# Softmax sums gathered by a longer chain of accumulating transfers, and a round's first two scores placed around its first transposed ones

## The chip, the cores and the metric

The kernel runs on one core of a Trainium2 chip. The metric is the device time of one execution in microseconds, as the median of several executions. The profile comes from one further execution; its instructions' span is a little shorter than that execution's time.

In the profile, PE is the matrix engine (PEld its weight loads), DVE the vector engine, ACT the scalar engine, POOL the GpSimd engine and SP the engine that issues most transfers.

## The reference

One pre-norm block over `x` of shape (2, 2048, 512), in float32: attention with 16 heads of 32 and two groups of keys and values, and then a feed-forward product with values rounded to an 8-bit format.

```python
x = x + attn(layernorm(x))
x = x + ffn(layernorm(x))

# attn: q, k with rotary positions
scores = einsum('bqhd,bkhd->bhqk', q * hd ** -0.5, k_exp) * hd ** -0.5
attn = softmax(scores, axis=-1)
out = einsum('bhqk,bkhd->bqhd', attn, v_exp).reshape(b, s, d)
return out @ wo + bo

# ffn: both operands rounded to e4m3 with one scale each
acc = matmul(x_fp8, w_fp8.T); return (acc * (sx * sw)).astype(bfloat16)
```

What matters here is the softmax: for each query and head, the maximum over 2048 keys, the exponentials, their sum over the keys, and the sum of values weighted by them.

## The kernel before

The tokens are cut into 8 blocks of 512 (four to a batch). A front part normalizes the first batch, projects its keys and values and the first queries. Then comes the attention loop, which takes nearly all of the time, and at the end the rounded product.

**Units.** The attention loop runs over 64 units. A unit is one block, one quad of four heads, and one half (256) of the block's queries. It runs in four rounds, and a round takes four chunks of 128 keys. The order of all instructions on each engine is the order of the program text (`tc.manual_schedule()`); nothing is reordered.

**Scores for the maxima (L517, L524).** A generator makes, for a later unit, plain scores `s` with queries on the partitions: 32 matmuls of 128x512 a unit, each followed by a maximum on DVE into `part`. Each call of `next(scores)` makes two. It runs eight scores ahead (`LEAD`), so a unit's loop makes the last 24 of the next unit's scores in its first three rounds, and the first eight of the unit after that in its last. The `s` tiles go round three banks of PSUM, of which one is at times lent to other work. After a unit's 32nd score the maxima are gathered (L531, L532), split into two parts on POOL (L503), and turned by PE (L542) ahead of the columns of chunk 14.

**Transposed scores and exponentials (L954, L963, L972).** In `probabilities`, PE makes transposed scores `T` (keys on the partitions, four heads of 256 queries) in two alternating banks, "E" and "O". In chunks 0 and 1 it first puts the negative maxima there by a selection matrix. `T` holds in later chunks only the difference of keys between chunks, added on top. ACT takes the exponential `p` (L972), in four buffers.

**Weighted values (L913).** `columns` multiplies the four chunks' `p` by the values, 16 matmuls a round, into one half of the bank `avs`.

**Sums of exponentials.** POOL adds the `p` of two chunks (`add_pair`, L946): the first two give `pair`, the last two a tile `pa` that is kept as `far_sums[r]`, with one buffer for each of the four rounds. A transfer that adds to its destination, issued by POOL (L1015), puts `pair` onto `far_sums[r]`; in the third round a second one (L1017) puts `far_sums[0]` onto `far_sums[1]`. In the next unit PE sums over the 128 partitions with a matrix of ones (`sum_up`, L927), into the other half of `avs`: `far_before[1:3]` at the end of the first round, `far_before[3:]` at the end of the second.

**End of the heads.** After the second `sum_up`, `finish_heads` is put into the list `finishing`. As a job it is stepped once when it is made, which has ACT copy the sums into `both[:, 1]` (L885). Its two reciprocals on DVE (L889) and the product on POOL (L890), which reads both halves of `both`, follow when `fill(ON_DVE)` reaches it, in the round after. The unit ends with ACT copying the weighted values into `both[:, 0]`:

```python
both = w2.tile([P, 2, HB], F32, tag="both", name=f"both_{u}", bufs=1)
nc.scalar.copy(both[:, 0, :], avs[:, 0, :])
far_before = far_sums
```

`both` has one buffer. In the next unit's text, ACT first has, in every other unit, a cast of queries (`hi_q`, L246, whose other half `lo_q` POOL makes, L247), and then the first exponentials.

**Other work.** Projections of keys and queries, the output product, the second normalization and the weight's rounding are jobs that `fill` steps between a round's parts: `fill(ON_PE)` after a round's second pair of scores (not in the first round) and ahead of its last pair, `fill(ON_DVE)` ahead of the columns.

Of the kernel before, what the change touches and what calls it, by code (L numbers as in the profile page):

```python
# [13 lines left out]
ALU = mybir.AluOpType  # L14
# [13 lines left out]
def preln_attn_fp8_ffn_kernel(  # L28
# [37 lines left out]
    nc = tc.nc  # L66
# [10 lines left out]
    HT = HB // P  # L77
    HALVES = TB // HB
    ROUND = 4
    ROUNDS = NTS // ROUND  # L80
    LEAD = 4

    ON_PE, ON_DVE, OTHER = "PE", "DVE", "other"
    LATER = "later"
# [24 lines left out]
    def s_bank():  # L109

        if s_next[0] == lent[0]:
            s_next[0] = (s_next[0] + 1) % S_BANKS
        tag = f"s{s_next[0]}"
        s_next[0] = (s_next[0] + 1) % S_BANKS
        return tag
# [354 lines left out]
    units = [(k, half) for k in range(len(quads)) for half in range(HALVES)]  # L470
# [23 lines left out]
    def group(k):  # L494
        return quads[k][1] // (QUADS // GROUPS)
# [11 lines left out]
    def scores_for_maxima():  # L507

        for u, (k, half) in enumerate(units):
            part = small.tile([P, HT, 4, NKB], F32, tag="part", name=f"part_{u}", bufs=3)  # L510

            order = [(i, kb) for i in range(HT) for kb in range(NKB)]
            for i, kb in order if u else sorted(order, key=lambda at: at[1]):
                for j in range(4):
                    s = ps_s.tile([P, TB], F32, tag=s_bank(), name=f"s_{u}_{i}_{kb}_{j}")
                    at = (half * HT + i) * P
                    nc.tensor.matmul(  # L517
                        s,
                        qst[k][:, j, at : at + P],
                        stacked["kS"][:, group(k), kb * TB : (kb + 1) * TB],  # L520
                        start=True,
                        stop=True,
                    )
                    nc.vector.tensor_reduce(part[:, i, j, kb : kb + 1], s, AX.X, ALU.max)  # L524
                    if j == 1:
                        yield u
                if (i, kb) == (HT - 1, NKB - 1):

                    mview = mrow.rearrange("p (i j r) -> p i j r", i=HT, j=4)
                    mx = small.tile([P, HT, 4], F32, tag="mx", name=f"mx_{u}")  # L530
                    nc.vector.tensor_reduce(mx, part, AX.X, ALU.max)  # L531
                    nc.scalar.copy(mview[:, :, :, 0], mx)  # L532
                    split.append((mview, mx))
                yield u
# [139 lines left out]
    def run(steps):  # L674
        for _ in steps:
            pass
# [4 lines left out]
    def together(*runs):  # L681

        live = list(runs)
        while live:
            for steps, n in list(live):
                for _ in range(n):
                    if next(steps, "end") == "end":
                        live.remove((steps, n))
                        break
# [9 lines left out]
    MIDDLE = DC + 1  # L699
    QUERIES = DC + 2  # L700
    scores = scores_for_maxima()
    PART = HT * 2
    with tc.manual_schedule():
        xnT = {
            0: wide_block("xnT", "xnT_kv_0"),
# [17 lines left out]
        kv[3] = project_kv(3, x_kv[3], xnT[3], load_tables(3))  # L723
        together((first(kv[3], FRONT), 2), (first(scores, PART), 1))
        together((first(kv[3], MIDDLE), 1), (first(scores, PART), 1))
        together((kv[3], 1), (first(scores, PART), 1))
        run(first(scores, PART))
        gather_maxima(0, ps_s.tile([P, TB], F32, tag=s_bank(), name="mtp_0"))
# [176 lines left out]
    def columns(u, chunks, probs, av):  # L905

        k, half = units[u]
        for kc, p in zip(chunks, probs):
# [3 lines left out]
            for j in range(4):  # L912
# [7 lines left out]
                    skip_group_check=True,  # L920
                )

    def sum_up(dst, parts, start, stop):

        for i, part in enumerate(parts):
            for j in range(4):
                nc.tensor.matmul(  # L927
                    dst[j * HD : (j + 1) * HD, :],
                    ones,
                    part[:, j, :],  # L930
                    start=start and i == 0,
                    stop=stop and i == len(parts) - 1,
                    tile_position=(0, j * HD),
                    skip_group_check=True,
                )
# [13 lines left out]
    def probabilities(u, T, kc):  # L949

        k, half = units[u]
        if kc < 2:
            for j in range(4):
                nc.tensor.matmul(  # L954
                    T[:, j, :],
                    sel[:, j, :],
                    maxima[u],
                    start=(j % 2 == 0),
                    stop=True,
                    skip_group_check=True,  # L960
                )
        for j in range(0, 4, 2):
            nc.tensor.matmul(  # L963
                T[:, j : j + 2, :],
                stacked["dkS"][:, group(k), kc * P : (kc + 1) * P],
                qst[k][:, j : j + 2, half * HB : (half + 1) * HB],
                start=False,
                stop=True,
                skip_group_check=True,
            )  # L970
        p = ppool.tile([P, 4, HB], F32, tag="p", name=f"p_{u}_{kc}")
        nc.scalar.activation(p, T, AF.Exp, scale=SCALE)  # L972
        return p

    with tc.manual_schedule():
        for _ in range(LEAD):
            next(scores)
        for u, (k, half) in enumerate(units):
            n, quad = quads[k]
            if half == 0 and quad == 0:  # L980
                attn_of[n] = wide.tile(
                    [P, QUADS, TB], F32, tag="attn", name=f"attn_{n}", bufs=2
                )
            stack_next(u)
            banks = [
                ps_t.tile([P, 4, HB], F32, tag="EO"[parity], name=f"T_{u}_{parity}")
                for parity in range(2)
            ]

            far_sums = []  # L990
            whole = u == len(units) - 1
            ending_soon = u >= len(units) - 2
            pieces = 2 if ending_soon else 1
            for r in range(ROUNDS):
                chunks = list(range(r * ROUND, (r + 1) * ROUND))
                step[0] += 1
                while r == 1 and landing:
                    landing.pop()()
                if r == 2:
                    ask(u)  # L1000
                last = r == ROUNDS - 1
                next(scores, None)
                probs = [probabilities(u, banks[kc % 2], kc) for kc in chunks[:2]]
                pair = add_pair(u, chunks[0], *probs)
                next(scores, None)
                if r > 0:
                    fill(ON_PE, pieces)
                probs.append(probabilities(u, banks[0], chunks[2]))
                next(scores, None)
                probs.append(probabilities(u, banks[1], chunks[3]))  # L1010
                if ending_soon:
                    fill(ON_DVE)
                if not (last and whole):
                    far_sums.append(add_pair(u, chunks[2], *probs[2:]))
                    nc.gpsimd.dma_start(out=far_sums[r], in_=pair, accum_op=ALU.add)  # L1015
                if r == 2:
                    nc.gpsimd.dma_start(out=far_sums[1], in_=far_sums[0], accum_op=ALU.add)  # L1017
                fill(ON_PE, pieces)
                next(scores, None)
                split_maxima()  # L1020
                fill(ON_DVE, 3 if finishing else 2)
                if r == 0:
                    avs = ps_av.tile([P, 2, HB], F32, tag="av", name=f"avs_{u}")
                columns(u, chunks, probs, avs[:, 0, :])


                if u > 0 and r == 0:
                    sum_up(avs[:, 1, :], far_before[1:3], False, False)
                elif u > 0 and r == 1:
                    sum_up(avs[:, 1, :], far_before[3:], False, True)  # L1030
                    finishing.append(Job(finish_heads(u - 1, both, avs[:, 1, :])))
            both = w2.tile([P, 2, HB], F32, tag="both", name=f"both_{u}", bufs=1)
            nc.scalar.copy(both[:, 0, :], avs[:, 0, :])
            far_before = far_sums
        sums = ps_s.tile([P, TB], F32, tag=s_bank(), name="sums_last")[:, :HB]
        sum_up(sums, [pair, *probs[2:], *far_sums[1:]], True, True)
        finishing.append(Job(finish_heads(u, both, sums)))
        fetch_y_over_keys(2, "kS", 1)
        attending[0] = False
        for jobs in (finishing, queue, beside):  # L1040
            while jobs:
                jobs[0].step()
                if jobs[0].kind is None:
                    jobs.pop(0)
# [55 lines left out]
    with tc.manual_schedule():  # L1100
# [5 lines left out]
        for at, (n, i) in enumerate(tiles):  # L1106
            if i % 2 == 0 and at + AHEAD < len(tiles):
                m, j = tiles[at + AHEAD]
# [58 lines left out]
```

## Time and profile before

| what | value |
|---|---|
| median of 3 runs | 2333.15 us (2331.62 to 2337.78) |
| the profiled execution | 2336.02 us |
| its span, first to last instruction | 2334.2 us |
| mean granted TensorE clock | 0.970 |
| L524 maxima on DVE | 1304.2 us, x2048 of 684 ns |
| L972 exponentials on ACT | 1001.4 us, x1024 of 1024 ns |
| L517 scores on PE | 832.1 us, x2048 |
| L963 transposed scores on PE | 669.5 us, x2048 |
| L913 weighted values on PE | 509.4 us, x8192 |
| L890 product on POOL | 85.2 us, x64 of 1331 ns |
| queue 0 (POOL's transfers) | 175.66 MB, 40.0% of 16 engines |
| queue 1 (SP's transfers) | 133.21 MB, 19.2% |
| transfers pa<-pa, issue to landing | median 4.9 us, longest 16.3 |

A row of groups gives the line, the engine, the operation, what it writes and reads, the count; then busy time and the mean of one; then the idle time of the engine just before and what ended it. In a timeline, the columns are the start, the length, the engine and the line, with idle time before it in brackets. A matmul on float32 values leaves two records. Records of POOL may overlap: an instruction can start before the record of the one ahead has ended.

### The profile page before, as it was taken

To read this page: it belongs to the slowest core of one execution; us is meant where nothing else is said; L and a number is where in the kernel's file an instruction comes from. 1 tells how busy PE (TensorE), PEld (TensorE's weight loads), DVE (VectorE), ACT (ScalarE), POOL (GpSimd) and SP (SyncE) were. 2 spreads that over 40 slices of the span, in tenths; PEclk is the share of its full clock that TensorE was granted. 3 is DMA by queue.
4 is the path that set the end of the run, shared out by engine and by line. 5 is a ranking of instruction groups with operands and counts; after the bars stand their busy time and mean duration, and the time that the engine had idled before them with its cause. 6 is when DMAs were issued, how large, how long until landed. Compare 5 with 4: busy or idle time off the path is not lost. (4 is left out here: it accounts for less than half of the span.)

```text
span 2334.2 us, 39403 instructions
## 1 busy us (share of the span) xinstructions
PE 2143.7 (92%) x15506; PEld 1242.2 (53%) x15506; DVE 1698.0 (73%) x2679; ACT 1237.0 (53%) x1545; POOL 1765.1 (76%) x1199
## 2 busy tenths in 40 slices
PE   5499999999999999999999999999999899899955
PEld 3255555555555555555555555555555455555522
DVE  3467778776777776876767778676877977767578
ACT  2146556655556555655445456555555555545646
POOL 3268889888878987888868878887888777877810
PEclk9599999999999999999999999999999999999978
DMA  6546656666465765659586456664665645847512
GB/s 204 160 102 128 141 114 161 140 142 131 100 163 130 159 129 136 145 115 197 103 202 137 102 127 136 147 112 96 133 154 123 138 101 115 170 98 197 109 52 112
DMA packets 116411, 312.78 MB, mean 134 GB/s; under 512 B 16896, under 2 KB 17536, under 8 KB 112384
## 3 DMA queue, kind: packets, MB, share of 16 engines
q0 software_dynamic: 50160, 175.66, 40.0%
q1 hardware_dynamic: 63648, 133.21, 19.2%
q8 instruction: 122, 2.00, 0.3%
q10 hardware_dynamic: 2416, 1.38, 0.2%
q14 instruction: 65, 0.53, 0.1%
HBM read 91.56 MB, written 42.99 MB: 58 GB/s over the span
## 5 line engine op out<-in xcount | busy, mean ns | idle before, releaser
L524 DVE TENSOR_REDUCE part<-s 128x1 f32<-128x512 f32 x2048 | 1304.2, 684 | 541.8 <-PE s L517 528.8
L946 POOL TENSOR_TENSOR pa<-p,p 128x1024 f32<-128x1024 f32 x511 | 1234.9, 2466 | 293.1 <-ACT p L972 265.8
L972 ACT ACTIVATE p<-T 128x1024 f32<-128x1024 f32 x1024 | 1001.4, 1024 | 597.8 <-PE T L963 564.6
L517 PE MATMUL s<-kS,qst 128*128 128x512 f32 x2048 | 832.1, 465 | 87.6 <-DVE part L524 28.7
L963 PE MATMUL T<-qst,dkS 128*128 128x512 f32 x2048 | 669.5, 423 | 11.8 <-ACT p L972 11.8
L517 PEld LDWEIGHTS s<-kS,qst 128*128 128x128 f32 x2048 | 369.7, 190 | 478.0 <-DVE part L524 266.5
L913 PE MATMUL avs<-p,vX 128*32 128x256 f32 x8192 | 509.4, 383 | 0.8 <-ACT p L972 0.8
L963 PEld LDWEIGHTS T<-qst,dkS 128*128 128x128 f32 x2048 | 366.0, 189 | 159.8 <-ACT p L972 54.8
L913 PEld LDWEIGHTS avs<-p,vX 128*32 128x32 f32 x8192 | 233.1, 109 | 214.4 <-issue 79.6
L1015 POOL DMA_DIRECT2D pa<-pa x255 | 224.2, 879 | 80.3 <-POOL pa L946 75.6
L301 PE MATMUL po<-wo_sb,attn 128*128 128x512 f32 x256 | 130.7, 596 | 1.3 <-POOL attn L890 1.3
L889 DVE RECIPROCAL both<-both 128x128 f32<-128x128 f32 x128 | 112.4, 920 | 11.2 <-ACT both L885 11.2
L301 PE MATMUL pq<-xnT_q,wq_sb 128*128 128x512 f32 x224 | 114.3, 592 | 0.0
L927 PE MATMUL avs<-pa,ones 128*32 128x256 f32 x1512 | 105.5, 382 | 5.5 <-DMA pa<-pa 5.5
L885 ACT COPY both<-avs 128x256 f32<-128x256 f32 x63 | 23.5, 372 | 132.8 <-PE avs L927 132.8
L890 POOL TENSOR_TENSOR attn<-both 128x256 f32<-128x256 f32 x64 | 85.2, 1331 | 5.9 <-DVE both L889 5.9
L954 PEld LDWEIGHTS T<-mT,sel 128*128 128x128 f32 x512 | 78.7, 190 | 13.6 <-ACT mT L546 1.9
L954 PE MATMUL T<-mT,sel 128*128 128x256 f32 x512 | 82.2, 283 | 1.1 <-ACT mT L546 1.1
L1017 POOL DMA_DIRECT2D pa<-pa x64 | 74.2, 1159 | 3.9 <-DMA pa<-pa 3.6
L927 PEld LDWEIGHTS avs<-pa,ones 128*32 128x32 f32 x1512 | 49.2, 111 | 38.6 <-DMA pa<-pa 6.0
L546 ACT CAST mT<-mtp 128x256 fp32r<-128x256 f32 x64 | 23.9, 373 | 84.0 <-PE mtp L542 84.0
L532 ACT CAST mrow<-mx 128x8 fp32r<-128x8 f32 x64 | 13.1, 205 | 93.5 <-DVE mx L531 93.5
(126 smaller groups left out, 1160.8 us busy)
## 6 DMA issues: line engine op xcount, KB each, us to landing
pa<-pa POOLq DMA_DIRECT2D x319, 512.0 KB, 4.9
qst<-q_far SPq DMA_DIRECT2D x128, 256.0 KB, 4.3
x_kv<-in_L_attn_x_dram SPq DMA_DIRECT2D x8, 1024.0 KB, 8.8
q_far<-hi_q SPq DMA_DIRECT2D x32, 256.0 KB, 4.4
q_far<-lo_q SPq DMA_DIRECT2D x32, 256.0 KB, 3.7
x_res<-in_L_attn_x_dram SPq DMA_DIRECT2D x8, 1024.0 KB, 8.2
x_res<-in_L_attn_bo_dram POOLq DMA_DIRECT2D x8, 1024.0 KB, 11.6
out_dram<-v SPq DMA_DIRECT2D x16, 512.0 KB, 2.8
```

Of the source, the lines that this page charges most:

```text
L301: nc.tensor.matmul(dst, lhs(c), rhs(c), start=(c == 0), stop=(c == chunks - 1))
L517: nc.tensor.matmul(s, qst[k][:, j, at : at + P], stacked["kS"][:, group(k), kb * TB : (kb + 1) * TB], start=True, stop=True,)
L524: nc.vector.tensor_reduce(part[:, i, j, kb : kb + 1], s, AX.X, ALU.max)
L889: nc.vector.reciprocal(piece, piece)
L890: nc.gpsimd.tensor_tensor(attn_of[n][:, quad, half * HB : (half + 1) * HB], both[:, 0, :], both[:, 1, :], ALU.mult)
L913: nc.tensor.matmul(av[j * HD : (j + 1) * HD, :], vX[batch(k)][:, kc, group(k), :], p[:, j, :], start=(kc == 0), stop=(kc == NTS - 1), tile ...
L927: nc.tensor.matmul(dst[j * HD : (j + 1) * HD, :], ones, part[:, j, :], start=start and i == 0, stop=stop and i == len(parts) - 1, tile_pos ...
L946: nc.gpsimd.tensor_tensor(pa, a, b, ALU.add)
L954: nc.tensor.matmul(T[:, j, :], sel[:, j, :], maxima[u], start=(j % 2 == 0), stop=True, skip_group_check=True,)
L963: nc.tensor.matmul(T[:, j : j + 2, :], stacked["dkS"][:, group(k), kc * P : (kc + 1) * P], qst[k][:, j : j + 2, half * HB : (half + 1) * H ...
L972: nc.scalar.activation(p, T, AF.Exp, scale=SCALE)
L1015: nc.gpsimd.dma_start(out=far_sums[r], in_=pair, accum_op=ALU.add)
```

## The change

Three things are done.

1. Sums: in a unit that follows one of the first 61, POOL issues two more accumulating transfers between its two adds of a round: in the first round `far_before[1]` onto `far_before[2]`, in the second `far_before[2]` onto `far_before[3]`. PE then sums only `far_before[3:]`, at the end of the third round. For the last three units' sums it stays as it was. `finish_heads` is made where the last `sum_up` is, so a round later.
2. Scores: the generator stops after every score instead of every second one (`LEAD` and `PART` are doubled to match). In the first round all stays in order; in the others, one of the first two scores goes ahead of the first transposed chunk and one between the first and the second.
3. In the front part, where the generator is interleaved with the projections step by step, a step is now one score.

```diff
-    LEAD = 4
+    LEAD = 8
...
                     nc.vector.tensor_reduce(part[:, i, j, kb : kb + 1], s, AX.X, ALU.max)
-                    if j == 1:
+                    if j < 3:
                         yield u
...
-    PART = HT * 2
+    PART = HT * 4
...
+    def in_one(u):
+
+        return 0 <= u < len(units) - 3
+
...
+    def more_scores(n):
+        for _ in range(n):
+            next(scores, None)
+
     with tc.manual_schedule():
-        for _ in range(LEAD):
-            next(scores)
+        more_scores(LEAD)
...
-                next(scores, None)
-                probs = [probabilities(u, banks[kc % 2], kc) for kc in chunks[:2]]
+                more_scores(2 if r == 0 else 1)
+                probs = [probabilities(u, banks[0], chunks[0])]
+                more_scores(0 if r == 0 else 1)
+                probs.append(probabilities(u, banks[1], chunks[1]))
                 pair = add_pair(u, chunks[0], *probs)
-                next(scores, None)
+
+                if r < 2 and in_one(u - 1):
+                    at = r + 2
+                    nc.gpsimd.dma_start(
+                        out=far_before[at], in_=far_before[at - 1], accum_op=ALU.add
+                    )
+                more_scores(2)
                 if r > 0:
                     fill(ON_PE, pieces)
                 probs.append(probabilities(u, banks[0], chunks[2]))
-                next(scores, None)
+                more_scores(2)
                 probs.append(probabilities(u, banks[1], chunks[3]))
...
                 fill(ON_PE, pieces)
-                next(scores, None)
+                more_scores(2)
                 split_maxima()
...
-                if u > 0 and r == 0:
+                if u > 0 and r == 0 and not in_one(u - 1):
                     sum_up(avs[:, 1, :], far_before[1:3], False, False)
-                elif u > 0 and r == 1:
+                elif u > 0 and r == (2 if in_one(u - 1) else 1):
                     sum_up(avs[:, 1, :], far_before[3:], False, True)
                     finishing.append(Job(finish_heads(u - 1, both, avs[:, 1, :])))
```

## The prediction

> **What bounds the kernel now.** I read the page first, then the groups by line, the source view of the one ACT copy that the change touches, and the timelines of single units. The page's groups:
>
> ```profile
> PE 2143.7 (92%) x15506; PEld 1242.2 (53%) x15506; DVE 1698.0 (73%) x2679; ACT 1237.0 (53%) x1545; POOL 1765.1 (76%) x1199
> ...
> L946 POOL TENSOR_TENSOR pa<-p,p 128x1024 f32<-128x1024 f32 x511 | 1234.9, 2466 | 293.1 <-ACT p L972 265.8
> ...
> L1015 POOL DMA_DIRECT2D pa<-pa x255 | 224.2, 879 | 80.3 <-POOL pa L946 75.6
> ...
> L927 PE MATMUL avs<-pa,ones 128*32 128x256 f32 x1512 | 105.5, 382 | 5.5 <-DMA pa<-pa 5.5
> ...
> L1017 POOL DMA_DIRECT2D pa<-pa x64 | 74.2, 1159 | 3.9 <-DMA pa<-pa 3.6
> ```
>
> PE sets the pace, but with many short waits (the list of waits has 266.5 us of L517's weight loads held by DVE). POOL, at 76% over the span, is nearer its limit inside a unit: over the 61 units that change, copy L1033 to copy L1033 in the timeline, a unit takes 32.9 us on average and POOL sits idle for 5.9 of them, in fourteen of them under 4. Where PE stands in a unit's first round, by the timeline of PE:
>
> ```profile
> 1644.89 1.93 PE L913 MATMUL avs<-p,vX 128*32 128x256 f32 x32
> 1646.64 1.05 PE L927 MATMUL avs<-pa,ones 128*32 128x256 f32 x16
> 1647.62 0.73 PE L517 MATMUL s<-kS,qst 128*128 128x512 f32 x2
> ```
>
> The sums (8 matmuls, two records each) hold PE for 0.98 us (1646.64 to 1647.62), while ACT and DVE wait for the next scores. That time is on the path.
>
> **What the change removes.** Those 16 records go in each of 61 units; the 8 records of the second round (0.55 us, 1653.91 to 1654.46) move to the third. Gain if nothing else answers: 61 x 0.98 = **-60 us** (by busy time 61 x 16 x 105.5/1512 = 68, an upper bound).
>
> **What it adds on POOL.** Two accumulating transfers a unit, each between a round's two adds. No row shows one there. From below: L1017 follows L1015 by 0.65 us (1663.29 to 1663.94 in the timeline further down). From above: L1015 with the gap before it, 0.30 + 0.88 = 1.18. It need not wait for the add ahead of it, so I take 0.75: 1.5 us of POOL a unit (1.3 to 2.4). Each is 512 KB; queue 0's 40.0% of 2334 us over its 327 issues is 2.86 us of all 16 engines, so 5.7 us more a unit. One unit (1034.69 to 1068.89) already shows a DMA share of 0.81 and would stand at 0.98; the span's mean is about 0.6.
>
> A link of the chain must wait until the one before has landed (median 4.9 us). The links lie a round apart, 6.4 to 9 us, and L1017, which waits in the same way, lost 3.6 us in 64 issues: I take 0, with +20 us as the far end, since one landing took 16.3.
> The Trainium skill speaks against a chain (DMA: Bandwidth & Descriptors, section "Rules for kernel authors"): the issuing engine has to wait for the completion semaphore of a transfer whose bytes the next one reads. The same page (section "Anatomy of one DMA") fits 2.0 us plus bytes over 436 GB/s, an estimate of 3.2 us a link; the trace's 4.9 decides. Either is shorter than a round, so both put the wait at nothing.
>
> **What it moves: the step that decides.** `finish_heads` is created a round later. Its reciprocals and the POOL product L890 run in the fill of the next round, so now in the unit's last. `both` has one buffer, and the unit ends with ACT copying into it (L1033). The source view of that line:
>
> ```profile
> L1033 ACT COPY both<-avs x64: 372/373/376, 158.5 to 2221.7; 128x256 f32<-128x256 f32 x64
> L1033 ACTq EVENT_SEMAPHORE  x63: 17/17/17, 188.9 to 2221.7; - x63
> ```
>
> From the second unit on the copy carries a second wait, which I read as the release of `both` by L890. Today L890 starts 2 to 8 us ahead of the copy, and the wait is over. A round later it lands behind the copy. POOL and then ACT at the end of such a unit:
>
> ```profile
> 1663.29 0.96 POOL L1015 DMA_DIRECT2D pa<-pa  x1 [0.30 <-POOL pa L946]
> 1663.94 1.21 POOL L1017 DMA_DIRECT2D pa<-pa  x1
> 1664.50 0.89 POOL L503 TENSOR_TENSOR mrow<-mx,mrow 128x8 fp32r<-128x8 f32 x1
> 1664.67 1.41 POOL L890 TENSOR_TENSOR attn<-both 128x256 f32<-128x256 f32 x1
> 1665.36 5.39 POOL L946 TENSOR_TENSOR pa<-p,p 128x1024 f32<-128x1024 f32 x2
> 1671.05 0.88 POOL L1015 DMA_DIRECT2D pa<-pa  x1 [0.30 <-POOL pa L946]
> ```
>
> ```profile
> 1667.13 0.38 ACT L546 CAST mT<-mtp 128x256 fp32r<-128x256 f32 x1 [1.02 <-PE mtp L542]
> 1668.22 0.38 ACT L1033 COPY both<-avs 128x256 f32<-128x256 f32 x1 [0.71 <-PE avs L913]
> 1669.79 2.94 ACT L972 ACTIVATE p<-T 128x1024 f32<-128x1024 f32 x3 [1.20 <-PE T L963]
> ```
>
> The product would follow the transfer of 1671.05, and the copy, now at 1668.22, would wait for it. Behind the copy on ACT stand the cast hi_q (every other unit) and the next unit's exponentials; for these wait PE's third scores T and then POOL's adds.
>
> *Quiet units* (POOL's last transfer ends within 1.6 us of the copy: 31 of 61). Take the one whose copy is at 1245.32. Transfer at 1245.38, +0.62 to the next instruction, product 1.38: 1247.4. Copy 0.37, hi_q 0.62: first exponential at 1248.4 instead of 1246.89, 1.5 late. PE's third T waits for its end (1249.4 for 1248.05), but PE's waits on DVE behind it (0.49, 0.41, 0.24) go, and the fourth T follows the second exponential's end at 1250.4 (1249.69): columns start 0.3 late. Less 0.98, -0.65; DVE's own work there (1252.65 to 1255.0) holds the next scores back, so I take -0.4 (0 to -0.9). 31 x -0.4 = **-12 us**.
>
> *Late units* (30): POOL still has adds when PE is done. Take copies at 1639.83 and 1668.22. In the first, the exponentials start 1.6 late, the columns 1.45 late, and the next round, less the sums, 0.5 late. On POOL the two links and that delay come on top, L890's 0.7 (1664.67 to 1665.36) goes: last transfer at about 31.05 after the copy, product 31.65 to 33.0. PE is ready at 28.5 (28.39 today), so ACT waits 4.5 us; the next unit starts its exponentials 3.4 late and gives back 1.0. Carried through the second unit in this way, copies drift by 2.1 us in two units: +1.05 each. Units in which POOL also turns keys or queries (32.94 us busy of 34.20 in the one named above) give 1.3 by the same steps. I take +1.1 (0 to 2.5). 30 x 1.1 = **+33 us**.
>
> A check: the loop now closed through POOL needs, besides its busy time, 2.5 us from the end of the product to the next add (copy 0.37, two exponentials 2.04), the gaps of today (5 x 0.3) and 1.5 for the links: 5.5 us a unit, less 1.3 where lo_q fills the restart. The shortfalls against the idle time of the 61 units add up to 34 us.
>
> **The scores on both sides of the first T** in three rounds of four. The first exponential may start one 128x512 matmul, 0.22 us, sooner. It pays only where PE's T waits for ACT: 158 times, 54.8 us (list of waits), so at most 158 x 0.22 = 35 us; DVE takes 0.65 us a score and mostly ends these waits next. From the other side, a second score 0.45 us later can cost DVE 0.1 in 183 rounds, +18. I take -5. In the front part the one-score steps only reorder (0, +-2 us).
>
> **Contention** of the 62 MB more, bounds 0 and +20 us: q_far's reads on SP's queue land in 4.3 us and are needed a unit later, so +3.
> The skill says that queues of SP and POOL share the same 16 DMA engines (same page, "Issuing engines are not separate DMA queues"). By that rule alone the 5.7 us more a unit would lengthen SP's loads in the unit at 0.81; no row here prices it.
>
> **Sum.** -12 + 33 - 5 + 3 = +19 us on the profiled execution's 2336.0 (span 2334.2 and 1.8 around it): 2355. The profiled execution lies 2.9 above the median 2333.2; taking half of that off, **2354 us**.
>
> **Rivals.**
> *The product is hidden* (0.19): if the second wait at L1033 is not the release of `both`, or PE's slack takes it up, late units gain like quiet ones: 61 x -0.98 = -60, 2273 us; with half of them gaining, 2303. For it: ACT is busy only 53%. It decides where L890 ends less than 1.1 us after PE's last column, for the exponential starts 1.57 after the copy and the copy takes 0.37. Against: in a quiet unit it ends 2.1 after it.
> *Even* (0.13): links at 0.65 and late units at +0.4: -12 + 12, 2333 us.
> *POOL as the full bound* (0.18), slower still: links at 1.18 plus waits for landings make the need 6.5 us; the shortfalls then come to 63, and with +20 of waits 2336 + 83 = 2419 us. It decides from a DMA share near 1 on. For it: the 0.81. Against: quiet units have 7 to 9 us of POOL idle.
> *The interleave decides*: 35 us at most, 2320; inside the first two. That the change does not do what it says would show in the counts: L927's records must fall to 61 x 8 + 2 x 24 = 536.
>
> **Chances.** The forecast (2340 to 2385) has 0.50; with the last rival slower has 0.68, within 0.3% 0.13 (2326 to 2340, about what a measurement here can tell from no change), faster 0.19. The likeliest case's own range is 2340 to 2385. For 8 in 10 I go to 2308 below, halfway into the hidden case, and 2400 above.
>
> **What would show it.** The copy L1033 waiting for POOL's L890, some 2 us in quiet units and 3 to 5 in late ones, 61 times; ACT's p after it late; POOL idle before L946 well under 293 us; PE's wait T on ACT up from 54.8 us; 122 more issues, landing near 5 us. If the copy does not wait, the forecast is wrong and the hidden case holds; if landings pass 7 us and POOL waits for DMA, the full bound does.

## The result, and the profile after

| | median, us | runs | ratio to before, 95% interval |
|---|---|---|---|
| before | 2332.4 | 2326.8 to 2337.8 | |
| changed | 2434.5 | 2431.4 to 2441.1 | 1.0437 [1.0421, 1.0452] |

The change costs 102 us. The forecast had the sign and the place of the main wait, but 2354 us, 21 more than the kernel before, and its range ended at 2400.

The page of the changed kernel (the columns are those of the lines shown before):

```profile
PE 2124.2 (87%) x14530; PEld 1233.5 (51%) x14530; DVE 1733.7 (71%) x2679; ACT 1228.8 (50%) x1545; POOL 1875.5 (77%) x1321
...
q0 software_dynamic: 67728, 239.63, 52.2%
...
L950 POOL TENSOR_TENSOR pa<-p,p 128x1024 f32<-128x1024 f32 x511 | 1277.3, 2542 | 211.5 <-ACT p L976 183.5
...
L1016 POOL DMA_DIRECT2D pa<-pa x122 | 108.0, 885 | 47.6 <-DMA pa<-pa 47.6
...
L1047 ACT COPY both<-avs 128x256 f32<-128x256 f32 x64 | 23.8, 372 | 212.1 <-POOL attn L890 202.7
...
L931 PE MATMUL avs<-pa,ones 128*32 128x256 f32 x536 | 43.5, 401 | 25.7 <-DMA pa<-pa 25.7
...
pa<-pa POOLq DMA_DIRECT2D x441, 512.0 KB, 5.2
qst<-q_far SPq DMA_DIRECT2D x128, 256.0 KB, 6.0
```

All that the change set out to do is there: the sums on PE fell from 1512 records to 536, and POOL issues 122 transfers more. PE's busy share fell to 87% all the same: it waits more. The new row is L1047, the copy that ends a unit. Its row before:

```profile
L1033 ACT COPY both<-avs 128x256 f32<-128x256 f32 x64 | 23.9, 373 | 43.3 <-PE avs L913 42.4 <-POOL pa L946 0.7
```

ACT had stood idle 43.3 us ahead of its 64 executions, for PE's columns; now it stands idle 212 us, and 202.7 of them end with POOL's product L890. The source view of the product says the same from its side:

```profile
L890 POOL TENSOR_TENSOR attn<-both x64: 725/1032/1377, 190.1 to 2326.5; 128x256 f32<-128x256 f32 x64
...
who waited for it (us, times):
  ACT both L1047: 202.7, 59
```

One such wait, in the timelines of POOL, ACT and PE in turn:

```profile
1742.12 0.87 POOL L1029 DMA_DIRECT2D pa<-pa  x1 [0.30 <-POOL pa L950]
1742.73 1.02 POOL L890 TENSOR_TENSOR attn<-both 128x256 f32<-128x256 f32 x1
```

```profile
1743.78 0.37 ACT L1047 COPY both<-avs 128x256 f32<-128x256 f32 x1 [4.78 <-POOL attn L890]
1744.05 1.95 ACT L976 ACTIVATE p<-T 128x1024 f32<-128x1024 f32 x2
```

```profile
1741.98 0.63 PE L517 MATMUL s<-kS,qst 128*128 128x512 f32 x2
1745.13 1.22 PE L967 MATMUL T<-qst,dkS 128*128 128x512 f32 x2 [2.53 <-ACT p L976]
1746.15 1.06 PE L517 MATMUL s<-kS,qst 128*128 128x512 f32 x2
```

The last transfer of the unit, the product right behind it, the copy 30 ns after the product, the exponentials right behind the copy; and PE, which has nothing left that it may do, stands still for 2.53 us. When it goes on, two 128x512 matmuls take 1.22 and 1.06 us where they took 0.63. The view of stretches shows the clock:

```profile
1738.50:1743.50 5.00, 4.11 (x33) 2.78 (x32) 4.46 (x7) 0.37 (x1) 4.70 (x4) 1.00 0.71 134
1745.10:1748.50 3.40, 3.37 (x8) 2.48 (x8) 1.29 (x2) 2.26 (x3) 2.42 (x2) 0.50 0.31 58
1748.50:1753.50 5.00, 4.98 (x44) 3.03 (x44) 4.83 (x8) 2.52 (x3) 4.02 (x3) 1.00 0.59 113
```

The columns are the stretch, its length, the busy time of PE, PEld, DVE, ACT and POOL, the granted clock, the DMA share and GB/s. The clock stood at 0.50 for 3.4 us. By the clock's records there are 29 such stretches between 160 and 2160 us, 126 us in all; before there were 4, 24 us.

From copy to copy, the 31 quiet units of the prediction took 13 us more together, the 30 late ones 85. In the last two units, which still sum in the old way, the copy starts 0.12 us after PE's last column, as before, and their times are within 0.4 us of before.

### The profile page after: what moved, and what is told of

Read it like the earlier page. It is cut to its first block, busy times and chain, and to the rows that moved or that the text cites. A ratio compares the mean times of both kernels' runs of the same rounds, so it can differ in the third digit from the quotient of the medians.

```text
span 2434.8 us, 37640 instructions
## 1 busy us (share of the span) xinstructions
PE 2124.2 (87%) x14530; PEld 1233.5 (51%) x14530; DVE 1733.7 (71%) x2679; ACT 1228.8 (50%) x1545; POOL 1875.5 (77%) x1321
## 4 chain that ended last, share of the span: by engine, by line
PE 35%; POOL 21%; DVE 16%; DMA 14%; ACT 7%; issue 5%; SPq 1%; DVEq 0%; ACTq 0%; POOLq 0%
POOL pa L950 13%; PE s L517 10%; DMA pa<-pa 10%; PE avs L913 9%; DVE part L524 9%; PE T L967 7%; ACT p L976 6%; PE po L301 3%; PE pq L301 3%; DVE sw_q L319 2%; POOL attn L890 2%; POOL pa L1029 1%; PE avs L931 1%; DMA qst<-q_far 1%; DMA sw_q<-q 1%
## 5 line engine op out<-in xcount | busy, mean ns | idle before, releaser
L524 DVE TENSOR_REDUCE part<-s 128x1 f32<-128x512 f32 x2048 | 1321.2, 686 | 602.6 <-PE s L517 597.9
L950 POOL TENSOR_TENSOR pa<-p,p 128x1024 f32<-128x1024 f32 x511 | 1277.3, 2542 | 211.5 <-ACT p L976 183.5
L517 PE MATMUL s<-kS,qst 128*128 128x512 f32 x2048 | 857.2, 467 | 102.3 <-DVE part L524 44.6
L967 PE MATMUL T<-qst,dkS 128*128 128x512 f32 x2048 | 725.1, 437 | 85.6 <-ACT p L976 84.5
L517 PEld LDWEIGHTS s<-kS,qst 128*128 128x128 f32 x2048 | 394.9, 195 | 468.9 <-DVE part L524 241.6
L913 PE MATMUL avs<-p,vX 128*32 128x256 f32 x8192 | 519.1, 387 | 10.1 <-ACT p L976 10.0
L967 PEld LDWEIGHTS T<-qst,dkS 128*128 128x128 f32 x2048 | 374.7, 195 | 247.4 <-ACT p L976 141.6
L1029 POOL DMA_DIRECT2D pa<-pa x255 | 223.2, 875 | 82.8 <-POOL pa L950 79.1
L1016 POOL DMA_DIRECT2D pa<-pa x122 | 108.0, 885 | 47.6 <-DMA pa<-pa 47.6
L1047 ACT COPY both<-avs 128x256 f32<-128x256 f32 x64 | 23.8, 372 | 212.1 <-POOL attn L890 202.7
L1031 POOL DMA_DIRECT2D pa<-pa x64 | 74.4, 1162 | 2.8 <-PE s L517 2.6
L890 POOL TENSOR_TENSOR attn<-both 128x256 f32<-128x256 f32 x64 | 66.3, 1036 | 8.9 <-DVE both L889 8.9
L885 ACT COPY both<-avs 128x256 f32<-128x256 f32 x63 | 23.5, 373 | 92.2 <-PE avs L931 92.2
L931 PE MATMUL avs<-pa,ones 128*32 128x256 f32 x536 | 43.5, 401 | 25.7 <-DMA pa<-pa 25.7
```

What stands on the lines that cost most here:

```text
L517: nc.tensor.matmul(s, qst[k][:, j, at : at + P], stacked["kS"][:, group(k), kb * TB : (kb + 1) * TB], start=True, stop=True,)
L890: nc.gpsimd.tensor_tensor(attn_of[n][:, quad, half * HB : (half + 1) * HB], both[:, 0, :], both[:, 1, :], ALU.mult)
L913: nc.tensor.matmul(av[j * HD : (j + 1) * HD, :], vX[batch(k)][:, kc, group(k), :], p[:, j, :], start=(kc == 0), stop=(kc == NTS - 1), tile ...
L950: nc.gpsimd.tensor_tensor(pa, a, b, ALU.add)
L967: nc.tensor.matmul(T[:, j : j + 2, :], stacked["dkS"][:, group(k), kc * P : (kc + 1) * P], qst[k][:, j : j + 2, half * HB : (half + 1) * H ...
L1016: nc.gpsimd.dma_start(out=far_before[at], in_=far_before[at - 1], accum_op=ALU.add)
```

## The experiments

Two theories. W: the copy's wait through the single buffer of `both`, with what follows from it, is the loss. L: the two links are, by their load on POOL and on the transfer engines. Line numbers differ by a few between the kernels; the copy is always the one that ends a unit. The kernel before was measured again beside each group of runs, with medians from 2333.0 to 2334.7 us, so differences of 2 or 3 us between groups say little.

**Two buffers for `both`.**

```diff
-            both = w2.tile([P, 2, HB], F32, tag="both", name=f"both_{u}", bufs=1)
+            both = w2.tile([P, 2, HB], F32, tag="both", name=f"both_{u}", bufs=2)
```

> The changed kernel with two buffers for `both` instead of one; nothing else differs. Theory W (the ACT copy at a unit's end waits for POOL's product through the one buffer of `both`, and this wait with what follows from it is the whole loss): the copy's wait on L890 (202.7 us, 59 times) falls to under 5 us, the granted clock returns to about 0.97, and the time falls by 100 us or more, to 2290 to 2335 us, at or under the kernel before. Theory L (the two added links load POOL and the transfer engines, and the wait is only where it shows): the wait goes, but ACT then waits for POOL at p or PE at the sums for a landing, and the time stays above 2380 us.

Measured: 2370.0 us, ratio 1.0154 [1.0139, 1.0169]. The second wait at the copy is gone: its separate semaphore instruction runs once instead of 63 times.

```profile
L1047 ACT COPY both<-avs x64: 372/372/375, 155.1 to 2256.6; 128x256 f32<-128x256 f32 x64
L1047 ACTq EVENT_SEMAPHORE  x1: 17/17/17, 2253.9 to 2253.9; - x1
```

That gives back 64 us, and 36 over the kernel before stay. Neither theory held: W missed by 35 us, L by 10. The list of waits of this run shows what stays:

```profile
ACT p L976 <- POOL pa L950: 97.1, 46, 8.0
...
PEld avs L931 <- DMA pa<-pa: 38.6, 10, 6.3
POOL pa L1016 <- DMA pa<-pa: 36.6, 15, 6.2
...
POOL pa L950 <- DMA pa<-pa: 34.3, 19, 5.1
```

The columns are the total, the number of times and the longest. ACT now waits for POOL's adds to free `p`, and POOL and PE wait for landings. The median landing of `pa` is 5.2 us, but the waits are few and long. In POOL's timeline, one of them, in a unit in which 1 MB loads are asked for:

```profile
403.75 0.87 POOL L1029 DMA_DIRECT2D pa<-pa  x1 [0.30 <-POOL pa L950]
406.84 2.33 POOL L950 TENSOR_TENSOR pa<-p,p 128x1024 f32<-128x1024 f32 x1 [2.22 <-DMA pa<-pa]
411.82 2.37 POOL L950 TENSOR_TENSOR pa<-p,p 128x1024 f32<-128x1024 f32 x1 [2.65 <-DMA pa<-pa]
```

By the releaser of the rows the adds wait for transfers: not for what they read, which comes from ACT, but for buffers that transfers still use. POOL takes its instructions in order, so all behind the add is late too. This unit (number 8, counted from 0) took 37.4 us from copy to copy, against 28.4 before.

**The late end alone**, with one buffer.

```diff
-                if r < 2 and in_one(u - 1):
-                    at = r + 2
-                    nc.gpsimd.dma_start(
-                        out=far_before[at], in_=far_before[at - 1], accum_op=ALU.add
-                    )
...
-                if u > 0 and r == 0 and not in_one(u - 1):
+                if u > 0 and r == 0:
```

> The changed kernel without its two links: PE sums far_before[1:3] in the first round as before, and far_before[3:] with the end of the heads in the third round as in the change. `both` has one buffer. So only the step that is a round later remains, and the scores around the first T. W: the copy waits for L890 about as before, 1.9 us in quiet units, 3 to 4 in late ones (150 to 200 us in all), and the time is 2380 to 2430 us. L: without the links the time is within 15 us of the kernel before, 2320 to 2345.

Measured: 2382.1 us, 1.0203 [1.0185, 1.022]. Without any link the copy still waits 191.2 us for the product:

```profile
L1042 ACT COPY both<-avs x64: 372/372/375, 158.7 to 2266.3; 128x256 f32<-128x256 f32 x64
L1042 ACTq EVENT_SEMAPHORE  x63: 17/38/38, 188.4 to 2266.2; - x63
its engine sat idle before it (us, times) until:
  POOL attn L890: 191.2, 59
```

So the wait needs no link, and costs some 54 us against the scores alone (2328.2, further down). W holds for this half.

**The links and the late end without the new placing of scores, and the new placing alone.**

```diff
-                more_scores(2 if r == 0 else 1)
+                more_scores(2)
                 probs = [probabilities(u, banks[0], chunks[0])]
-                more_scores(0 if r == 0 else 1)
```

> The changed kernel with a round's first two scores together ahead of the first T again; the links and the late end of the heads stay. W and L: the placing of the scores is worth little either way, 2420 to 2445 us. Rival I (the scores around the first T hold DVE back and cost several tenths of a microsecond a round): under 2405 us.

```diff
-        return 0 <= u < len(units) - 3
+        return False
```

> The kernel before with only the scores around the first T and the one-score steps of the generator; sums and end of the heads as before. W and L: 2315 to 2335 us, at most 20 us gained, nothing lost. Rival I: over 2345 us.

Measured: 2422.9 us (1.0379 [1.0364, 1.0395]) and 2328.2 us (0.9972 [0.996, 0.9984]). Both lie in the range of W and L. The placing gains 5.5 us alone, and in the changed kernel it loses 11.6.

**Links that carry almost nothing**, in the kernel with two buffers.

```diff
-                        out=far_before[at], in_=far_before[at - 1], accum_op=ALU.add
+                        out=far_before[at][:, 0, :8],
+                        in_=far_before[at - 1][:, 0, :8],
+                        accum_op=ALU.add,
```

> The kernel with two buffers of `both` (2370 us), with both links still issued in each unit but carrying only 8 of a tile's 1024 columns, so that most of far_before[1] and far_before[2] is left out of the sums. Instructions on POOL, semaphores and PE's work stay; the data is gone. Theory D (what is left of the loss is the data: links land late behind other loads, and POOL, PE and ACT wait for the landing): POOL's and PE's waits for landings (36.6, 34.3 and 33.8 us) fall near those of the kernel before, and the time is 2285 to 2320 us. Theory P (POOL's time for issuing 122 more transfers is what is left): 2345 us or more.

Measured: 2329.9 us, 0.9984 [0.9971, 0.9996]: 40 us less than with full links, 10 above what D gave and 15 below P. In its list of waits the waits for landings fell, and the wait for POOL's adds did not:

```profile
ACT p L976 <- POOL pa L950: 117.1, 64, 6.0
...
POOL pa L950 <- DMA pa<-pa: 23.1, 12, 3.9
...
POOL pa L1016 <- DMA pa<-pa: 11.0, 8, 3.0
```

The data of the links costs 40 us. Unit by unit, in the profiles, that cost lies in the even units (49.5 us longer with the data), in which SP moves queries; the odd ones are 6.3 us shorter. What the issues alone cost, with these short waits for almost empty transfers in it, the run without links, further down, measures.

**Links in odd units only**, two buffers.

```diff
-        return 0 <= u < len(units) - 3
+        return 0 <= u < len(units) - 3 and u % 2 == 0
```

> The kernel with two buffers of `both`, with the two links only in the second unit of each pair (odd units); in the even ones, in which SP writes and reads back the next queries, the sums go to PE in the first and second round as before. Taken unit by unit from the traces, odd units were 20.9 us shorter with links than with the scores alone (2328 us), even ones 65.2 us longer. D: 2298 to 2318 us, faster than both kernels. P (every link costs alike): about halfway, 2340 to 2360 us.

Measured: 2319.5 us, 0.994 [0.9923, 0.9956], 1.5 us above D's figures and far from P's. The odd units, without SP's query traffic, are 20.7 us shorter than with the scores alone. But 13.7 of these come with the late end of the heads by itself (the run of the late end with two buffers, further down), so a gain by the links isn't shown here, only that they cost nothing in these units.

**Matmuls that only keep PE busy**, in the changed kernel with its one buffer.

```diff
                 more_scores(2)
+                if r == 0 and u - 1 in LATE:
+                    keep_busy(u)
...
+    def keep_busy(u):
+        s = ps_s.tile([P, TB], F32, tag=s_bank(), name=f"busy_{u}")
+        k, half = units[u]
+        for i in range(8):
+            nc.tensor.matmul(
+                s,
+                qst[k][:, i % 4, half * HB : half * HB + P],
+                stacked["kS"][:, group(k), :TB],
+                start=True,
+                stop=True,
+            )
```

> The changed kernel (one buffer of `both`), with eight 128x512 matmuls into a spare bank of scores ahead of the third T of the first round, in the 24 units that follow a long wait of the copy; they compute nothing that is used, 1.7 us a unit and 41 in all if nothing hides them. Theory C (a wait of more than some 2 us lets PE stand idle, the granted clock falls to half for 3.4 or 6.8 us, and this adds to the loss): stretches at half clock in the loop fall from 29 to under 18, and the time falls by 10 us or more, under 2425 us. Rival: the half clock costs nothing of its own, since PE waits then anyway: 2434 us or more.

`LATE` holds the 24 units that end with a long wait. Measured: 2421.4 us, 1.0373 [1.0357, 1.0389]. More work, 13 us less time. The copy waits as long as ever (207.1 us for L890), but by the clock's records there are 14 stretches at half clock (75 us) for 29 (126 us), and the mean granted clock is 0.964 for 0.949:

```profile
core 0: 2416.3 us, clock 0.964
```

The added matmuls feed nothing that is used, so the gain is put down to the clock: the half clock has a price of its own. The 13 us are what half of the stretches cost, less what the added matmuls take; the price of all stays unmeasured, as 14 remain. The Trainium skill (TensorE: Matmul & The Clock Gate, section "HAM oscillation — how this bites in real kernels") puts the limit at idle gaps over some 3.4 us. Here a gap of 2.53 us was enough. In the changed kernel PE has 30 pauses of 2 to 3.4 us from 160 to 2290 us, and by the clock's records a stretch at half clock starts in 24 of them or up to 1.5 us behind; the measurement decides. The length of the pause alone doesn't settle it: after this one of 2.69 us the clock stayed at 1.00.

```profile
2228.20:2230.89 2.69, 0.00 (x1) 0.00 (x1) 1.09 (x2) 1.35 (x3) 1.30 (x2) 1.00 0.66 126
2230.89:2235.89 5.00, 5.00 (x44) 3.12 (x45) 3.94 (x8) 2.78 (x3) 4.06 (x3) 1.00 0.28 52
```

**Two buffers, scores in pairs** (the edits of the first and the third experiment together).

> The kernel with two buffers of `both` (2370 us), with a round's first two scores together ahead of the first T as in the kernel before; the links stay. The scores around the first T gained 5.5 us alone and lost 11.6 us in the changed kernel. If that loss hangs on the copy's wait: 2370 to 2380 us. If it hangs on the links (exponentials start sooner and wait for POOL): 2355 to 2366 us.

Measured: 2366.7 us, 1.0144 [1.0122, 1.0166], between the two expectations and not to be told from 2370.0. The 11.6 us that the placing lost are mostly gone with the copy's wait; why it lost there isn't settled.

**PE's saving by itself**: two buffers, no links, and the sums of far_before[1:3] left out.

> The kernel with two buffers of `both` (2370 us) without the two links, and without the sums of far_before[1:3] on PE, so that only far_before[3] reaches the sums and three quarters of the exponentials are left out of them. It measures what PE's 976 records alone are worth, the term of -60 us. If they are all on the path: 2328 - 60, 2265 to 2280 us; with the tiny links at 2330 us, issuing 122 transfers on POOL then costs some 55 us. Rival (PE's time there is refilled by other waits): 2300 us or more.

Measured: 2278.8 us, 0.9762 [0.9743, 0.978], in the range of the first case. But that range started from the scores alone (2328). Against the next run, which has the late end too, the saving is 39 us and not 60.

**The late end with two buffers, without links.**

> The kernel without links whose heads end a round later (2382 us with one buffer of `both`), now with two buffers. W: the later end costs nothing but the copy's wait, so the time is that of the scores alone, 2320 to 2338 us. Rival (a later end also disturbs DVE and POOL by its reciprocals and product in the last round): 2350 us or more.

Measured: 2317.9 us, 0.9934 [0.9913, 0.9955], 64 us less than with one buffer, and 2 under W's range. So the late end costs nothing but the wait. It even gains 10 us on the scores alone; by the profiles they lie in the odd units, and what gains them stays open.

**Links in odd units from number 9 on**, two buffers.

```diff
-        return 0 <= u < len(units) - 3 and u % 2 == 0
+        return 8 <= u < len(units) - 3 and u % 2 == 0
```

> The kernel with links in odd units only (2320 us), now without them in the first eight units, where POOL also turns the second batch's first keys and queries: there the units added up to 259.6 us against 252.3 with the scores alone. 2308 to 2318 us if these units fall back to 252; 2318 us or more if the first eight are slow for another cause.

Measured: 2311.2 us, 0.9906 [0.9889, 0.9924]: faster than both kernels, 22 us under the one before. It is the fastest of the kernels that make all the sums. In its profile the first eight units took 252.5 us, as expected. With links in 27 units it is 7 us under the kernel without any (2317.9), and the intervals overlap; that kernel also ends all heads late. That this one beats the kernels before and after is clear, that the links still help in it isn't.

**The account.** Each step is the difference of two medians of runs that differ in that alone (in the second row also in the second buffer, which takes the wait away):

| step | from, to, us | us |
|---|---|---|
| scores around the first T | 2333.7, 2328.2 | -5.5 |
| end of the heads a round later, no wait | 2328.2, 2317.9 | -10 |
| PE without the sums of far_before[1:3] | 2317.9, 2278.8 | -39 |
| issuing two more transfers a unit on POOL, almost empty | 2278.8, 2329.9 | +51 |
| their data | 2329.9, 2370.0 | +40 |
| one buffer of `both` | 2370.0, 2434.5 | +64 |
| sum | 2333.7, 2434.5 | +101 |

Each step holds the half clock that goes with it: the 29 stretches of the changed kernel are 16 with two buffers. The step of the buffer was measured on two paths, with links (64) and without (2382.1 to 2317.9, 64). And the chain of links doesn't pay for itself even without the copy's wait: it gives back 39 us and takes 91.

## Why the prediction was wrong in size and right about the wait

**The step that decides** was the right one. The second wait at the copy is the release of `both` by L890: it goes with a second buffer and comes with the late end alone. Its lengths were foreseen, about 2 us in quiet units and 3 to 5 in late ones; from PE's last column to the copy they are 2.2 and 3.8 on average. The signs named beforehand came: L1047 waits for L890, POOL's idle time before its adds fell from 293 to 211 us, PE's weight loads of T wait 141.6 us for ACT instead of 54.8, the median landing is 5.2 us. The sum was +19 us and the runs have +101. Two parts of it make up the difference of 82: the links' landings and contention miss by 37, the quiet and late units together by 45.

**The single term that failed most** is that of the links' landings and of contention, 0 and +3 us, where +40 was measured. The prediction compared the median landing, 4.9 us, with the 6.4 to 9 us from link to link and found no wait. The median hardly moved. The waits are in the tail, as the list of waits of the changed kernel shows:

```profile
POOL pa L1016 <- DMA pa<-pa: 47.6, 21, 5.4
...
PEld avs L931 <- DMA pa<-pa: 30.8, 10, 5.7
POOL pa L950 <- DMA pa<-pa: 26.8, 17, 4.4
```

At L1016, 20 of the 21 waits are the second link's, which must wait until the first has landed: the very wait that was taken as 0. Of POOL's 38 waits, 36 fall in even units, and so do all of PE's: units in which SP moves queries or 1 MB blocks. Before, POOL's adds waited 6 times for 16.2 us. The prediction named the unit with a DMA share of 0.81 and the longest landing of 16.3 us, and yet priced the term by the median. It also named a median over 7 us as the sign of the worse case, which never came.

**The quiet units**, -12, and the **late ones**, +33, failed as a sum: +21 was forecast and +66 measured, from the steps +64 (the buffer), +51 (the issues), -39 (PE's saving) and -10 (the late end). In the forecast's terms they held 60 us of saving against 81 of cost. PE's saving was mis-sized: alone it is worth 39 us. Where the other 21 went wasn't isolated; without the sums ACT waits 32.4 us for POOL's adds, where it waits 13.6 with them. On the side of the cost, POOL's two issues take 0.42 us of the kernel's time each (51 us over 122), waits of 11.0 us at L1016 included; the prediction let their 1.5 us a unit disappear in POOL's idle time in all quiet units. And the half clock after PE's longer waits wasn't foreseen at all; its whole price stays open.

**The scores around the first T**: -5 foreseen, -5.5 measured, if nothing else is changed. The -5 was picked between -35 and +18, so much of that is luck, and in the changed kernel the same edit costs 11.6 us.

**The rivals.** POOL as the full bound (2419 us) came nearest in size and for half the right reason, waits for landings. But it needed a DMA share near 1; the kernel with two buffers shows 0.78 from 160 to 2160 us and the loss in single units. The hidden product did not come about.

## What to carry to other kernels

A step that is moved later runs into the reuse of its buffers: look for the next writer of each tile that it reads, on whichever engine, before counting what the move saves. Here a second buffer of 2 KB a partition was worth 64 us. Price a transfer that a queue must wait for by its landing beside the largest loads, not by its median. And count an in-order engine's issues as time of that engine, even where it looks idle a sixth of the time.

## What the hardware showed that was not expected

After most of PE's pauses of 2 to 3.4 us, 24 of 30 in the changed kernel, its granted clock stands at 0.50 for 3.4 or 6.8 us, and in the stretch shown two matmuls take 1.22 us for 0.63. Eight matmuls of no use where such a pause falls, in 24 units, made the kernel 13 us faster.
